# A graph kernel whose degrees are counted with ScalarE's one-hots, and whose first norms and messages are spread out

## The chip, the cores and the metric

The kernel runs on one core of one Trainium2 chip. The metric is the time of one launch on the device in microseconds (us). The core has five engines that run side by side and wait for each other by semaphores: TensorE (PE; its weight loads are shown apart as PEld), VectorE (DVE), ScalarE (ACT), GpSimd (POOL) and SyncE (SP). Each runs its instructions in the order in which they stand in its queue.

## The reference: what is computed

There are 6250 nodes with 128 features and 100000 edges, sorted by their destination. Each edge has a source, a destination and one of 8 types. First comes a relational graph network of three layers. In a layer, each edge fetches the row of its source under its type, weighs it by one over the number of edges that share its destination and type, and adds it to its destination:

```
h = einsum('ni,rio->nro', x, weight)        # one row per node and type
msg = h[src, etype]
norm = 1.0 / max(count of edges with the same (dst, etype), 1)
agg = segment_sum(msg * norm, dst)
x = agg + x @ root + bias                   # then batch norm and relu, but for the last layer
```

Between the two networks, and behind the second, a sum with the input is normalized by rows. The second network has no types and works with the degrees of the sources:

```
deg = segment_sum(1, src)
w = rsqrt(deg[src]) * rsqrt(deg[dst])
repeat 3 times: cur = segment_sum(cur[dst] * w, src); acc += cur
out = (acc / 4) @ W_out + b_out
```

## The kernel before

**The tiles.** The edges stand in 782 tiles of 128 (NTS). The first 192 (HT) belong to the first destinations, where many edges meet. Of these, tiles 0 to 91 (T1) are not gathered: dense_sums() (L1325) works them off as a multiplication with a table of counts. Tiles 92 to 191 are summed by first_sums() (L1087), and tiles 192 to 781 by window_sums() (L1644).

**A pass.** Each of the three layers is one pass. Its first part is first_sums(): for each of 100 tiles, GpSimd starts an indirect DMA (L1064) that fetches 128 rows of x into one of 27 buffers named gt, PE multiplies them with weighted one-hots o (L1067), which DVE makes for eight tiles at a time (one_hots(), L1052), and DVE adds the product to z (joined(), L1095). Beside it run the messages (messages(), L968): for each of 49 blocks of nodes two multiplications of 512 columns (L972), each copied by ScalarE (L973), and a store of 512 KB on SP's queue (L974) into the table h_d in DRAM; behind them 13 multiplications with root (L985). `nodes` is this generator, stepped in proportion to the tiles done: all 62 steps over the first `HN` = 66 tiles. The second part is window_sums(): 590 tiles, gathered from h_d, so it needs all the stores. Its products are added to agg (L1655). Between the passes stands a batch norm (L1697 to L1719).

**The norms.** The weight of each edge needs counts along rows of sorted edges. shares() (L814) is a chain of some 70 DVE operations with comparisons, scans in both directions and a few transposes by PE. It runs twice: for the edges of the first 208 tiles ("x", on rows of 256, L938), and for all the edges (on rows of 1024) within others() (L1031), a generator of 33 steps that also makes the gather indices gidx and the local columns lo. In layer 0 others() is stepped once per tile of first_sums(), from the fifth tile on (beside_layer_0, L1118). weights() (L674) makes the weight of a layer out of four bases, in 32 DVE operations of 128 columns.

**Work for later, beside the gathers.** The tables that dense_sums() and the last part need are built meanwhile by side_work() (L1613), a generator that window_sums() steps by take_turns() (L1640) in proportion to the tiles, over all three passes. It has three parts:

- hot_counts() (L1156): 62 steps for the table c1_d of the first destinations. dense_sums() needs it, which begins after 400 tiles of a pass's second part (DENSE_FROM).
- degrees() (L1404): how many edges each source has. For each of 196 groups of four tiles (TS), DVE compares 128 columns (lo_hot, L1419) and 49 columns (blk_hot, L1422) with the two parts of the source's number, both as one-hots of bf16, and PE multiplies the one with the other (L1431), adding up all 782 tiles in one PSUM tile pd. dis, the inverse root, is made of it.
- counts() (L1443): 12 steps of setting up with long DVE operations and PE multiplications in fp32 (L1507, L1529), then 1232 steps, one for each tile of a reordered list: a row (L1587), one-hots dst_hot for four tiles (L1583), two PE multiplications (L1601), an addition (L1560), and a store to a_d.

Before, one step of hot_counts() is followed by three of degrees(); then come the rest of degrees() and counts(). pd is also the sixth accumulator of dense_sums(), so degrees() must have ended before the first dense_sums() (L1674).

**The last part** (from L1736) multiplies with the table a_d, three times, and normalizes.

**What sets the order.** The program is written as generators, but a scheduler of the framework lays out each engine's queue: an instruction goes ahead as soon as its operands are expected. pin() (L749) ties an instruction to the pinned one before it on the same engine, so that pinned instructions keep the order of the text. Before, the one-hots, the gather multiplications, the joined additions and the steps of the side work are pinned; shares(), others(), checks() and weights() are not. GpSimd's queue holds almost nothing but gathers, in the order of the tiles.

Of the kernel before, what the change touches and what calls it, by code (L numbers as in the profile page):

```python
# [17 lines left out]
P = 128  # L18
# [501 lines left out]
def sorted_path(  # L520
# [60 lines left out]
    HW = 7  # L581
# [10 lines left out]
    DENSE_FROM = 400  # L592

# [163 lines left out]

    def rsqrt(pool, o, v, shape, name):
# [55 lines left out]
    def shares(x_, q, w, dst_x_, typ, to, j, meanwhile):  # L814
# [6 lines left out]
        nc.vector.tensor_tensor(same, dst_x_[:, : w + 1], dst_x_[:, 1:], op=OP.is_equal)  # L821
        nc.vector.tensor_scalar(at_first, at, at[:, 0:1], None, op0=OP.is_equal)
        yield
        nc.vector.tensor_scalar(at_last, at, at[:, w - 1 : w], None, op0=OP.is_equal)
        nc.vector.tensor_scalar(pair, typ, 2.0, None, op0=OP.is_ge)
        yield
        for k in range(2, KP):
            nc.vector.scalar_tensor_tensor(pair, typ, 2.0 * k, pair, op0=OP.is_ge, op1=OP.add)
        yield
        nc.vector.scalar_tensor_tensor(odd, pair, -2.0, typ, op0=OP.mult, op1=OP.add)  # L830
        nc.vector.tensor_scalar(unit, odd, 4095.0, 1.0, op0=OP.mult, op1=OP.add)
        yield
        ms = [m0, m1, m2, m3]
        for k, m in enumerate(ms):
            nc.vector.memset(m[:, w:], 0.0)
            nc.vector.scalar_tensor_tensor(m[:, :w], pair, float(k), unit, op0=OP.is_equal, op1=OP.mult)
            if k % 2:
                yield
        edge_cnt = [sp.tile([q, KP], F32, name=f"edge_cnt{x_}{k}") for k in range(2)]
        through = [sp.tile([q, KP], F32, name=f"through{x_}{k}") for k in range(2)]  # L840
        for i, mask in ((0, at_last), (1, at_first)):
            for k in range(KP):
                u = sp2.tile([P, W], F32, name="u")[:q, :w]
                nc.vector.scalar_tensor_tensor(u, ms[k][:, :w], 1.0, mask, op0=OP.mult, op1=OP.mult,
                                               accum_out=edge_cnt[i][:, k : k + 1])
                if k % 2:
                    yield
            nc.vector.tensor_tensor(through[i], at_last[:, 0:1].to_broadcast([q, KP]),
# [9 lines left out]
        for k in range(2):  # L858
            pq = pqs[k]
            flow = sp.tile([KP, 2 * P], F32, name=f"flow{x_}{k}")  # L860
            nc.vector.tensor_copy(flow.rearrange("p (k q) -> p k q", k=2)[:, :, :q],
                                  pq.rearrange("p (k q) -> p k q", k=2)[:, :, :q])
            run = sp.tile([KP, q + 2], F32, name=f"run{x_}{k}")
            nc.vector.memset(run, 0.0)
# [3 lines left out]
            nc.vector.tensor_tensor_scan(to_, keep, add, 0.0, op0=OP.mult, op1=OP.add)  # L868
            if k == 0 and w == W:

                full = sp.tile([KP, q], F32, name="full")
                nc.vector.scalar_tensor_tensor(full[:, : q - 1], keep[:, : q - 1], 1.0, keep[:, 1:],
# [8 lines left out]
        for k in range(2):  # L881
            b = sp.tile([q, KP], F32, name=f"before_row{x_}{k}")
            nc.vector.tensor_copy(b, pbs[k])
            before_row.append(b)
        meanwhile(2)
        for k in range(KP):
            f = sp2.tile([P, W], F32, name="u")[:q, :w]
            b = sp2.tile([P, W], F32, name="u")[:q, :w]
            nc.vector.tensor_tensor_scan(f, same[:, :w], ms[k][:, :w], before_row[0][:, k : k + 1], op0=OP.mult,
                                         op1=OP.add)  # L890
            yield
            nc.vector.tensor_tensor_scan(b[:, ::-1], ms[k][:, w:0:-1], same[:, w:0:-1],
                                         before_row[1][:, k : k + 1], op0=OP.add, op1=OP.mult)
            yield
            nc.vector.tensor_tensor(f, f, b, op=OP.add)
            if k == 0:
                nc.vector.scalar_tensor_tensor(total, pair, float(k), f, op0=OP.is_equal, op1=OP.mult)
            else:
                nc.vector.scalar_tensor_tensor(f, pair, float(k), f, op0=OP.is_equal, op1=OP.mult)
                nc.vector.tensor_tensor(total, total, f, op=OP.add)  # L900
# [3 lines left out]
        nc.vector.tensor_copy(hi_i, total)  # L904
        nc.vector.tensor_scalar(hi_i, hi_i, 12, None, op0=OP.logical_shift_right)
        nc.vector.tensor_copy(hi, hi_i)
        yield
        nc.vector.scalar_tensor_tensor(low, hi, -4096.0, total, op0=OP.mult, op1=OP.add)
        nc.vector.tensor_sub(hi, hi, low)
        yield  # L910
        nc.vector.tensor_mul(hi, hi, odd)
        nc.vector.tensor_add(total, low, hi)
        nc.vector.tensor_scalar_max(total, total, 1.0)
# [4 lines left out]
        nc.vector.reciprocal(to, to)  # L918
# [76 lines left out]
    def checks():  # L995

        skip = wide_tiles["at_last"][:Q, :W]
        nc.vector.scalar_tensor_tensor(skip, dst_f[:, :W], 0.0, dst_f[:, 1 : W + 1], op0=OP.add,
# [951 lines left out]
```

## Time and profile before

| what | us |
|---|---|
| median of 3 runs (3580.69 to 3591.91) | 3583.28 |
| the profiled execution | 3580.38 |
| its span | 3578.5 |
| first gather from h_d in layer 0, 1, 2, at | 199.66, 1184.71, 2119.13 |
| busy in the span: PE, DVE, ACT, POOL | 2714.5, 2272.8, 324.2, 2114.9 |
| last gather, at | 2879.17 |

A group of the profile is one line of the kernel on one engine: its operation, what it writes and reads, how often, its busy time and its mean in ns; behind the second bar the time for which the engine stood idle just before it, with what it waited for. A line of the timeline gives the start, the duration, engine, line and operation, and in brackets the idle time before it. A line of the windows gives busy time and number of instructions of each engine in one stretch, then the granted clock of PE as a share of full speed, the share of the DMA engines and GB/s. A line of the waits gives the sum, how many there were, and the longest.

### The profile page before, as it was taken

How to read it: one execution, taken by the hardware profiler on the slowest of the kernel's cores; microseconds unless marked ns; L12 is line 12 of the kernel's file. 1: busy time of each engine (PE TensorE's matmuls, PEld its weight loads, DVE VectorE, ACT ScalarE, POOL GpSimd, SP SyncE). 2: the span in 40 equal slices, each digit the busy share in tenths (PEclk: the TensorE clock that was granted, in tenths of full speed). 3: DMA queues.
4: the chain of work that ended last, by engine and by line, in shares of the span. 5: the costliest groups of instructions: out<-in, count | busy, mean ns of one | idle time of the engine just before them, and what ended most of it. 6: DMA issues, size and time to landing. Idle time of an engine off the chain costs nothing.

```text
span 3578.5 us, 53292 instructions
## 1 busy us (share of the span) xinstructions
PE 2714.5 (76%) x17110; PEld 2167.3 (61%) x17110; DVE 2272.8 (64%) x6623; ACT 324.2 (9%) x600; POOL 2114.9 (59%) x2083
## 2 busy tenths in 40 slices
PE   5976667677659766666765986666677679999998
PEld 3464455655545555555544565555555569999997
DVE  7678896953752766666456357666653566656566
ACT  3500000001025000000100520000001020000000
POOL 6577777677757777777776667777777710000000
PEclk9955556558569555555765985555567579999999
DMA  6611122123238222222322852222233234545442
GB/s 194 230 52 50 52 61 70 45 66 97 59 115 313 64 66 68 68 71 73 100 69 58 297 184 78 76 77 78 76 86 79 68 97 135 158 131 157 133 139 80
DMA packets 422807, 373.23 MB, mean 104 GB/s; under 512 B 89934, under 2 KB 370286, under 8 KB 422516
## 3 DMA queue, kind: packets, MB, share of 16 engines
q1 hardware_dynamic: 347832, 230.32, 21.0%
q0 software_dynamic: 66240, 135.79, 13.5%
q10 hardware_dynamic: 8444, 3.61, 0.4%
q8 instruction: 136, 2.23, 0.3%
q14 instruction: 155, 1.27, 0.1%
HBM read 250.74 MB, written 178.62 MB: 120 GB/s over the span
## 4 chain that ended last, share of the span: by engine, by line
PE 39%; DMA 37%; DVE 11%; issue 7%; POOL 5%; DVEq 0%; POOLq 0%; ACT 0%; ACTq 0%
DMA gt<-h_d,gidx 37%; PE pw L1865 15%; PE pw L972 7%; PE ps L1067 6%; POOL gt L1064 5%; PE pw L1368 3%; PE pw L1601 2%; DVE row L1587 2%; DVE had L1560 1%; PE pw L1395 1%; PE pw L985 1%; DVE dst_hot L1583 1%; DVE agg L1655 1%; PE ps L1823 1%; PE pd L1368 1%
## 5 line engine op out<-in xcount | busy, mean ns | idle before, releaser
L1064 POOL DMA_INDIRECT gt<-h_d,gidx x1770 | 1797.9, 1016 | 554.1 <-DMA gt<-h_d,gidx 221.8
L1067 PE MATMUL ps<-o,gt 128*128 128x48 f32 (+1 forms) x4140 | 1148.3, 391 | 666.8 <-DMA gt<-h_d,gidx 590.9
L1067 PEld LDWEIGHTS ps<-o,gt 128*128 128x128 f32 x4140 | 947.5, 290 | 954.2 <-DMA gt<-h_d,gidx 779.2
L1587 DVE TENSOR_SCALAR row<-iota_c,e_tab,e_tab 128x252 bf16<-128x252 int16 x1232 | 421.6, 350 | 326.2 <-PE pw L1601 324.3
L1865 PE MATMUL pw<-three,u 128*128 128x193 bf16 x7203 | 615.8, 248 | 14.2 <-issue 9.9
L1865 PEld LDWEIGHTS <-u 128*128 128x128 fp8e3 x7203 | 602.4, 98 | 21.8 <-issue 10.0
L1601 PE MATMUL pw<-dst_hot,row 128*126 128x128 bf16 x2464 | 411.9, 318 | 56.8 <-DVE row L1587 51.9
L1601 PEld LDWEIGHTS <-row 128*126 128x126 bf16 x2464 | 337.1, 225 | 74.3 <-DVE row L1587 64.1
L1560 DVE SCALAR_TENSOR_TENSOR had<-had,keep,pw 126x256 int32<-126x256 int32 x616 | 292.1, 474 | 1.9 <-PE pw L1601 1.8
L972 PE MATMUL pw<-w,xT 128*128 128x512 f32 x588 | 288.8, 622 | 0.0
L1064 POOL DMA_INDIRECT gt<-x_d,xidx x200 | 195.0, 975 | 133.7 <-DMA xc<-in_x_dram 31.9
L1655 DVE TENSOR_TENSOR agg<-agg,ps 128x48 f32 x885 | 178.6, 202 | 141.6 <-PE ps L1067 107.3
L1859 DVE TENSOR_SCALAR u<-packed 128x640 int32<-128x640 int32 (+1 forms) x243 | 127.0, 522 | 201.9 <-PE pw L1865 200.1
L1583 DVE TENSOR_TENSOR dst_hot<-iota_f,e_tab 128x512 bf16<-128x512 f32 x308 | 211.5, 687 | 0.0
L1095 DVE TENSOR_TENSOR z<-z,ps 128x56 f32 x300 | 63.0, 210 | 194.2 <-PE ps L1067 182.3
L973 ACT COPY hs<-pw 128x512 f32<-128x512 f32 x294 | 171.7, 585 | 141.3 <-PE pw L972 134.4
L1368 PE MATMUL pw<-x,u 128*128 128x385 bf16 x735 | 178.3, 385 | 6.6 <-DVE had L1560 3.3
L1064 POOL DMA_INDIRECT gt<-in_x_dram,xidx x100 | 119.3, 1193 | 77.3 <-PE ps L1067 46.3
L972 PEld LDWEIGHTS pw<-w,xT 128*128 128x128 f32 x588 | 106.1, 197 | 86.9 <-issue 80.7
L1419 DVE TENSOR_TENSOR lo_hot<-iota_f,e_tab 128x512 bf16<-128x512 f32 x196 | 134.3, 685 | 32.4 <-PE pd L1431 31.3
L1368 PEld LDWEIGHTS <-u 128*128 128x128 fp8e3 x882 | 101.3, 119 | 79.7 <-issue 40.5
L1056 DVE TENSOR_TENSOR o<-iota_f,lo 128x384 f32<-128x384 f32 x222 | 122.7, 553 | 41.0 <-PE ps L1067 41.0
(396 smaller groups left out, 1890.8 us busy)
## 6 DMA issues: line engine op xcount, KB each, us to landing
a_d<-had SPq DMA_DIRECT2D x616, 126.0 KB
h_d<-hs SPq DMA_DIRECT2D x147, 512.0 KB
packed<-a_d SPq DMA_DIRECT2D x135, 320.0 KB
packed<-a_d SPq DMA_DIRECT2D x108, 384.0 KB
gt<-h_d,gidx POOLq DMA_INDIRECT x1770, 2.5
c_d<-had SPq DMA_DIRECT2D x62, 196.0 KB
packed<-c_d SPq DMA_DIRECT2D x21, 448.0 KB
x_d<-xc SPq DMA_DIRECT2D x24, 256.0 KB
```

The costliest lines, as they stand in the source:

```text
L972: nc.tensor.matmul(ph, xT[:, b * P : (b + 1) * P], w[:, c : c + 512], start=True, stop=True)
L973: nc.scalar.copy(hs[:, c : c + 512], ph)
L1064: nc.gpsimd.indirect_dma_start(out=gt, out_offset=None, in_=table[:, :], in_offset=bass.IndirectOffsetOnAxis(ap=at[:, t : t + 1], axis=0))
L1067: pin(nc.tensor.matmul(pa, gt, o, start=first_, stop=last))
L1368: nc.tensor.matmul(sums[d][:, :C3D], us[d % 2][:, i, :, d // 2], x3[:, i, :], start=(c == 0 and i == 0), stop=(c * CH + i == NBLK - 1))
L1419: pin(nc.vector.tensor_tensor(hot[:, :n, :], iota_f[:, None, :].to_broadcast([P, n, P]), src_lo[:, t0 : t0 + n, None].to_broadcast([P, n, P]),
L1560: pin(nc.vector.scalar_tensor_tensor(now[:HB, : 2 * P], had[:HB, : 2 * P], keep[:HB, s : s + 1], p[:HB, : 2 * P], op0=OP.mult, op1=OP.add))
L1583: pin(nc.vector.tensor_tensor(hots[i // TS], iota_f[:, None, :].to_broadcast([P, TS, P]), flat(e_lo)[:, i : i + TS, None].to_broadcast([P, ...
L1587: pin(nc.vector.tensor_scalar(rows[i][:, : 2 * HB], iota_c[:, : 2 * HB], e_col[:, s, j : j + 1], e_val[:, s, j : j + 1], op0=OP.is_equal, ...
L1601: pin(nc.tensor.matmul(sums[s][:HB, c * P : (c + 1) * P], row[:, c * HB : (c + 1) * HB], hots[u // TS][:, u % TS, :], start=(j == 0 and c ...
L1655: pin(nc.vector.tensor_add(to, to, pa))
L1865: nc.tensor.matmul(out_of(f), bytes_[f % 2][:, d, :, f // 2], cur[:, b, :], start=(b == 0 and f % 2 == 0), stop=(c0 == NSL - 1 and d == m ...
```

## The change

Four things are changed.

1. degrees() makes its one-hots on ScalarE: the absolute difference of a column number and the source's part, for 128 and for 49 columns of one tile (Abs), then one Relu of 1 minus that for four tiles. It sums DEG = 4 groups (16 tiles) in pd at a time and adds pd to deg on DVE. It works in two halves of the tiles, and uses the memory of e_src.
2. side_work() leaves hot_counts() at one step in four, with nothing in the other three, then starts counts(), and steps degrees() once per step of counts() from step 12 on. dense_sums() waits for an open group of degrees() only (close_degrees).
3. In layer 0 the messages and the root multiplications spread over HT - T1 - 8 = 92 tiles instead of 66, and others() is stepped in two of five tiles instead of in each.
4. All DVE operations of shares(), checks(), others() and of the first weights are pinned by `in_order`. The first weights are made by 7 operations of 1024 columns.

In the next layers the messages still take 66 tiles.

```diff
+    class Pinned:
+        def __getattr__(self, name):
+            return lambda *args, **kw: pin(getattr(nc.vector, name)(*args, **kw))
+
+    in_order = Pinned()
...
-        nc.vector.tensor_tensor(same, dst_x_[:, : w + 1], dst_x_[:, 1:], op=OP.is_equal)
+        in_order.tensor_tensor(same, dst_x_[:, : w + 1], dst_x_[:, 1:], op=OP.is_equal)
...
-    w0 = weights(0, bases_0)
+    w0 = wp.tile([P, R * D], F32, name="w")
+    w0_r = w0.rearrange("p (r d) -> p r d", r=R)
+    comp_0 = comp_b[:, : R * NB].rearrange("p (r b) -> p r b", b=NB)
+    for b in range(NB):
+        to = w0_r if b == 0 else sp2.tile([P, W], F32, name="u").rearrange("p (r d) -> p r d", r=R)
+        in_order.tensor_tensor(to, bases_0[:, b, None, :].to_broadcast([P, R, D]),
+                               comp_0[:, :, b, None].to_broadcast([P, R, D]), op=OP.mult)
+        if b:
+            in_order.tensor_tensor(w0_r, w0_r, to, op=OP.add)
...
     def beside_layer_0(k):
-        for _ in range(1 if k >= 4 else 0):
+        if k >= 4 and k % 5 in (0, 2):
             next(other_tiles, None)
 
-    first_sums(0, layer_0, NBLK + NC, HN, beside_layer_0)
+    first_sums(0, layer_0, NBLK + NC, HT - T1 - 8, beside_layer_0)
...
     def degrees():
...
+        HALF = -(-NTS // 2)
+        room = flat(e_src)
+        src_lo, src_blk = room[:, :HALF], room[:, HALF : 2 * HALF]
+        for h in range(2):
+            of = gidx[:, h * HALF : h * HALF + HALF]
...
+            for t0 in range(begin, end + TS, TS):
+                n = min(TS, end - t0)
+                if n > 0:
+                    near = cp.tile([P, TS, P + NBLK], BF16, name="near")
+                    for j in range(n):
+                        k = t0 - begin + j
+                        nc.scalar.activation(near[:, j, :P], iota_b, AF.Abs, bias=src_lo[:, k : k + 1], scale=-1.0)
+                        nc.scalar.activation(near[:, j, P:], iota_b[:, :NBLK], AF.Abs,
+                                             bias=src_blk[:, k : k + 1], scale=-1.0)
+                        yield
+                    nc.scalar.activation(near[:, :n, :], near[:, :n, :], AF.Relu, bias=ones[:, :1], scale=-1.0)
+                    made[t0] = near, n
+                if t0 > begin:
+                    near, n = made.pop(t0 - TS)
+                    step = (t0 - TS - begin) // TS
+                    first_, last = step % DEG == 0, step % DEG == DEG - 1 or t0 >= end
+                    if first_:
+                        pd = ps_d.tile([P, 512], F32, name="pd")
+                    for j in range(n):
+                        pin(nc.tensor.matmul(pd[:, :NBLK], near[:, j, :P], near[:, j, P:],
+                                             start=first_ and j == 0, stop=last and j == n - 1))
+                    if last:
+                        if h == 0 and step < DEG:
+                            pin(nc.vector.tensor_copy(deg, pd[:, :NBLK]))
+                        else:
+                            pin(nc.vector.tensor_add(deg, deg, pd[:, :NBLK]))
+                    open_degrees[0] = not last
...
     def side_work():
-        others = degrees()
         for _ in hot_counts():
+            for _ in range(3):
+                yield
+        counted[0] = True
+        others = beside[0] = degrees()
+        for k, _ in enumerate(counts()):
+            if k >= 8 + 2 * TU:
+                next(others, None)
             yield
-            for _ in range(3):
-                if next(others, "end") != "end":
-                    yield
-        counted[0] = True
         for _ in others:
             yield
-        degrees_known[0] = True
-        for _ in counts():
-            yield
-    N_SIDE = 6 + NS1 + 2 + 2 + -(-NTS // TS) + 1 + 5 + 2 * TU + 3 + NST * TU + LEAD
+
+    def close_degrees():
+        while open_degrees[0]:
+            next(beside[0])
+
+    N_SIDE = 3 * (6 + NS1 + 2) + 5 + 2 * TU + 3 + NST * TU + LEAD
...
                 finish_sums[0]()
-                assert counted[0] and degrees_known[0]
+                close_degrees()
+                assert counted[0]
                 dense = dense_sums(l, w)
```

## The prediction, made before the changed kernel was run

> **What bounds the kernel now.** The page first: GpSimd (POOL) is busy only 59% of the span, but those 2115 us lie ahead of about 2880 us, where the multiplications of the last part (L1865) begin.
>
> ```profile
> span 3578.5 us, 53292 instructions
> ...
> PE 2714.5 (76%) x17110; PEld 2167.3 (61%) x17110; DVE 2272.8 (64%) x6623; ACT 324.2 (9%) x600; POOL 2114.9 (59%) x2083
> ...
> L1064 POOL DMA_INDIRECT gt<-h_d,gidx x1770 | 1797.9, 1016 | 554.1 <-DMA gt<-h_d,gidx 221.8
> ```
>
> All but a few of POOL's waits in front of a gather are 0.3 us long (221.8 us are 728 waits, the longest 0.3), which is what one gather needs before the next: POOL was not held up, it is the bound. In the timeline of POOL the 590 gathers from h_d take 823 us in layer 0 (199.66 to 1023), 767 in layer 1 (1184.71 to 1951) and 761 in layer 2 (2119 to 2880). The same work is 57 us dearer in layer 0, and the windows show where:
>
> ```profile
> core 0: us, PE busy (x) PEld busy (x) DVE busy (x) ACT busy (x) POOL busy (x), PEclk, DMA share, GB/s
> 57.00:168.00 111.00, 102.26 (x300) 51.28 (x301) 80.72 (x159) 58.06 (x100) 57.47 (x52) 0.92 0.70 259
> 215.00:585.00 370.00, 238.48 (x1440) 182.43 (x1440) 325.18 (x869) 2.67 (x4) 291.99 (x256) 0.50 0.20 57
> 1185.00:1690.00 505.00, 339.33 (x1594) 279.97 (x1594) 346.77 (x1018) 0.00 (x0) 386.77 (x389) 0.50 0.25 69
> ```
>
> From 215 to 585 us, while degrees() runs, a gather comes every 370/256 = 1.445 us; in layer 1, beside counts(), every 505/389 = 1.298 us. VectorE (DVE) is 88% and 69% busy there, ScalarE (ACT) nearly idle. The groups of POOL in these two windows give the gather itself:
>
> ```profile
> L1064 POOL DMA_INDIRECT gt<-h_d,gidx x256 | 292.1, 1141 | 78.0 <-DMA gt<-h_d,gidx 39.3 <-issue 25.6 <-PE ps L1067 6.7
> L1064 POOL DMA_INDIRECT gt<-h_d,gidx x389 | 387.2, 995 | 118.5 <-DMA gt<-h_d,gidx 44.8 <-issue 34.4 <-PE pw L1601 31.7
> ```
>
> An undisturbed gather takes 0.94 us. The timeline shows what stretches one: this one began at 551.16, and DVE ran one comparison with two inputs in SBUF after the other, without a pause:
>
> ```profile
> 551.03 0.68 DVE L1419 TENSOR_TENSOR lo_hot<-iota_f,e_tab 128x512 bf16<-128x512 f32 x1
> 551.64 0.35 DVE L1422 TENSOR_TENSOR blk_hot<-iota_f,e_tab 128x196 bf16<-128x196 f32 x1
> 551.91 0.68 DVE L1419 TENSOR_TENSOR lo_hot<-iota_f,e_tab 128x512 bf16<-128x512 f32 x1
> ...
> 551.16 3.73 POOL L1064 DMA_INDIRECT gt<-h_d,gidx  x1 [0.30 <-DMA gt<-h_d,gidx]
> ```
>
> It ended only after 554.57, when DVE came to an operation that reads PSUM (L1312).
>
> **A rule weighed against this.** The Trainium skill, "SBUF — State Buffer", section "Who interferes with whom", has VectorE and GpSimd share one pair of ports, locked by either for a whole instruction; it names tensor_tensor with both inputs in SBUF. Taken by the letter, the lock is free again after every instruction, so a gather could lose at most one comparison, 0.69 us: with 382 of them over 256 gathers and half an operation (0.26 us) lost each time at 55% of DVE's time, some 0.14 us per gather, or 37 us. The row shows 2.79 us lost at once under a closed run of them, so loss goes by runs, not by instructions. Both leave the excess at 256 x (1.445 - 1.298) = 38 us; they differ on what is left when DVE stays nearly as busy with other work, and there layer 1's 1.298 is measured, so I use that.
>
> **The change, part by part.**
>
> *Degrees' comparisons leave DVE.* 196 x (0.687 + 0.355) = 204 us of DVE work go, nearly all between 211 and 573 us. hot_counts() keeps its one step in four turns, now with nothing in the other three, and counts() starts some 215 tiles into the pass instead of some 270; after that a turn holds one step of counts(), 1457/1460 = 1.00 against 1516/1460 = 1.04 before, so layer 0 gets the DVE mix that layer 1 has. 590 x 1.300 = 767 us. On top comes what layer 1 doesn't have, the setting up of counts(): PE runs 92 fp32 multiplications in a row (592 to 645 us) and POOL waited 15.0 us for a buffer. The planned order of the changed kernel has that run unbroken as well, with four short operations of degrees() more in DVE's queue (about 2 us): 17 us. Slow first tiles beside the set-up of hot_counts(), +5; then hot_counts() alone, 210 tiles at an estimated 0.02 us less than beside counts() (DVE some 2.7 us in 5.2 instead of 69%), -4. So 785 instead of 823: **38 us gained** (30 to 50).
>
> *ScalarE takes them.* 782 tiles, each an Abs of 128 and one of 49 columns, and a Relu of 708 for four tiles. The nearest rows have a bias per partition too:
>
> ```profile
> L991 ACT ACTIVATE agg<-pw,bias_c 128x512 f32<-128x512 f32 x12 | 8.2, 687 | 4.8 <-PE pw L985 4.8
> ...
> L991 ACT ACTIVATE agg<-pw,bias_c 128x128 f32<-128x128 f32 x1 | 0.4, 359 | 0.0
> ```
>
> That is 0.25 us and 0.85 ns per column: 0.36 + 0.29 + 0.86/4 = 0.86 us per tile, 676 us in all, against a tile's 1.30 us. ScalarE has no other work inside a pass (0.00 in the window of layer 1), so all of it is hidden; POOL, PE and DVE do not wait as long as it stays under 1.30. Lower bound, 0.20 us for an Abs (bn_a, one column, L762): 0.6 us per tile; upper bound, 0.687 for an Abs: 1.6, which would be 784 x 0.3 = 235 us lost. The 128-column row is the very width, so I take 0.86. The page "ScalarE: Activation LUTs", section "Rules for kernel authors", speaks against the change: relu and the like belong on VectorE, up to three times faster per element. Here it is 0.26 us on DVE against 0.86 on ACT, so by the rule the change loses 782 x 0.6 = 470 us of engine time. It is no loss of span: DVE's 0.26 stretches the bound engine, ACT's 0.86 touches nothing.
>
> *PE's part* stays 782 multiplications at about 0.07 us pitch (four in 0.37 to 0.53 us), now one tile in each turn: PE goes from 67% to some 73% in these stretches. PE's order is fixed, so it would stand at a near tile that is late; the Relu is placed a group of four (5.2 us) ahead of its multiplications and ScalarE needs 3.5 us for a group: cost 0, covered by 27 buffers, 35 us of gathers.
>
> *49 additions of PSUM into deg* on DVE, 0.2 us each (agg, L1655), 10 us in all. Each waits for the PE's newest multiplication; behind it on DVE stand the next row (L1587) and the had addition. DVE has 0.4 us of slack per turn, 6 us per 16 tiles; a wait of 1 to 3 us fits: 0. On SP the 62 stores of c1_d and the 616 of a_d keep their order; the last of c1_d leaves near 465 us, and dense_sums() reads it after 400 tiles, near 700 us: 0. The finishing of an open group ahead of dense_sums() is at most 16 tiles of ScalarE, 14 us, twice: under the 35 us. At the end of layers 0 and 1 up to 16 tiles of ScalarE stand ahead of the first hs copies, and the load of the square root's table comes in layer 0's normalization: 0 to 2 us each, 2 in all.
>
> *First pass of layer 0.* Its 100 gathers end at 199.66, though 100 x 1.29 would be 129 us. POOL's waits there:
>
> ```profile
> POOL gt L1064 <- PE ps L1067: 47.2, 28, 13.1
> ```
>
> PE frees the buffers late, because it makes the messages (busy 102 of the 111 us of the first window above): the last of 196 halves ended at 168.0, and POOL, at gather 76 then, needed 25 more. PE's sum from the start of messages (57.5) is 98 x 0.857 + 37 tiles x 0.33 + transposes 2 = 98 us; 12 more are waits. In the changed order all 49 transposes of x come before anything else, the chain for the first norms is 5 us shorter (18 foreign operations leave it, 6 us, and pinning costs 1), w is 7 x 1.2 us instead of 32 short operations (10 us), but DVE stands some 8 us at the zeroing of the last x buffer. Messages start near 49.5; the 16 tiles that PE did before them (7.4 us) come later. Last message: 49.5 + 84 + 56 x 0.33 + 2 = 154, with 0 to 13 us of waits, taken as 5: 159. By then 56 tiles are freed instead of 52, POOL is at gather 83, and 17 x 1.45 later (DVE's chain of 76 us now lies beside the last gathers) the first gather from h_d goes out at 184 to 187. SP's stores of h_d end 20 us earlier than that and are no bound. The norms are ready near 184: their readers are PE's window tiles, with 27 gathers of cover. **13 us gained** (-5 to 20).
>
> Sum against the profiled execution (3580.4 us; 3578.5 of span and 1.9 around it): -38 - 13 + 2 - 2 (layers 1 and 2 with 4% fewer DVE steps, 58 us of excess over 0.94) = -51. The median shown is 2.9 us above that execution, so 3583.3 - 51 = **3532**.
>
> **Rivals.**
> 1. *The pins bite.* With one fixed order on DVE and on PE, each waits for the other in the first 200 us: tiles 72 to 99 stand behind the norm chain, whose scans are 2.4 us each. The 13 us are lost or turn to -9: 3545 to 3563, about 3554. For it: PE already waits 16.1 us for a norm (L913) at the start. Against: only 17 gathers lie behind it. Chance 0.16.
> 2. *The change does not lighten the gathers*: counts() in the first pass locks as much as degrees() did, pitch near 1.42. Then 13 us remain: 3570. Against it stand 390 gathers of layer 1. Chance 0.07.
> 3. *Slower: ScalarE becomes the pace.* If one tile costs it x > 1.30 us, PE stands at each group (queued behind it: the gather multiplications, and for their buffers POOL), 784 x (x - 1.30) us. From x = 1.365 it eats the 51 us. With the fixed part of an activation doubled to 0.5 us, x is 1.43 and the time 3583 + 102 - 51 = 3634. Against: 0.86 from the rows. Chance 0.09.
>
> **How the numbers follow.** Likeliest 0.68, own range 3515 to 3548 (gathers 30 to 50, first pass 5 to 20). The range goes up to rival 1's end and a part of rival 2 and down to both gains at their best, 3510 to 3568. A difference within 0.3% (11 us) is about what a measurement of this kernel can't tell from no change. Faster: likeliest, rival 1 and half of rival 2, 0.87; within: 0.05; slower: 0.08.
>
> **What would show it.** Right: 590 gathers from h_d of layer 0 in 775 to 795 us, with a mean near 1.0 us and no gather over 2.5 us between 220 and 560; the first one near 185; ACT busy near 1000 us, each tile about 0.8 us; layers 1 and 2 unchanged within 5 us; the last part from L1865 on as long as before. Wrong: PE waiting for ACT at the degrees' multiplications in total over 50 us, a pitch over 1.36 in layer 0, or a first gather from h_d after 200 us.

## The result and the profile after

The changed kernel takes 3529.2 us (median, 3523.1 to 3530.6), the kernel before 3585.8 us beside it: a ratio of 0.9837, 95% interval 0.9825 to 0.985. The forecast was 3532. All ratios below are to the kernel before, run beside the kernel in question on the same chip; but for one chip its median was 3585.6 to 3586.5 us. The profiled execution has a span of 3528.1 us against 3578.5. First the page of the changed kernel, its span, busy times and the row of the gathers (busy and mean ns, then the idle time before them):

```profile
span 3528.1 us, 54660 instructions
...
PE 2695.5 (76%) x17110; PEld 2161.4 (61%) x17110; DVE 2125.9 (60%) x6259; ACT 916.4 (26%) x2360; POOL 2083.9 (59%) x2083
...
L1080 POOL DMA_INDIRECT gt<-h_d,gidx x1770 | 1768.9, 999 | 546.8 <-DMA gt<-h_d,gidx 235.6
```

DVE lost 147 us of work, ACT took on 592 (916.4 - 324.2), and a gather became 17 ns shorter on average. GpSimd (POOL) still sets the pace: most of its waits in front of a gather are again 0.3 us (us in total, times, longest):

```profile
POOL gt L1080 <- DMA gt<-h_d,gidx: 235.6, 773, 0.3
```

Its timeline, cut at the first and last gather of each pass, shows where 50 us went:

| stretch on POOL, us | before | forecast | after |
|---|---|---|---|
| start to first gather from h_d | 199.7 | 184 to 187 | 182.7 |
| 590 gathers from h_d, layer 0 | 823.4 | 785 | 783.1 |
| boundary to layer 1 | 31.6 | up to +2 | 32.6 |
| x gathers, layer 1 | 130.1 | same | 127.9 |
| 590 gathers from h_d, layer 1 | 766.7 | about -1 | 775.0 |
| boundary to layer 2 | 31.9 | up to +2 | 32.0 |
| x gathers, layer 2 | 135.8 | same | 136.0 |
| 590 gathers from h_d, layer 2 | 761.0 | about -1 | 757.7 |
| rest | 698.4 | same | 701.0 |

Layer 1 is the one row that went the other way. The windows of the changed kernel: the first two as in the prediction, the last one the stretch of layer 1 in which degrees() now runs beside counts():

```profile
core 0: us, PE busy (x) PEld busy (x) DVE busy (x) ACT busy (x) POOL busy (x), PEclk, DMA share, GB/s
57.00:168.00 111.00, 106.42 (x376) 58.31 (x374) 82.92 (x153) 58.58 (x100) 78.00 (x63) 0.97 0.71 264
215.00:585.00 370.00, 261.36 (x1081) 195.45 (x1079) 246.06 (x708) 54.78 (x164) 278.67 (x275) 0.54 0.22 62
...
1140.00:1655.00 515.00, 358.65 (x1984) 303.62 (x1984) 343.99 (x1015) 303.29 (x895) 395.81 (x392) 0.50 0.24 68
```

In the first window POOL makes 63 gathers where it made 52. In the second DVE is busy 67% instead of 88%, and a gather comes every 370/275 = 1.345 us instead of 1.445; the window holds the setting up of counts(), so it is not the steady pace, which is 320/246 = 1.30 from 640 to 960 us. In layer 1 it comes every 515/392 = 1.314, against 1.298 before, although DVE is less busy (66.8% against 68.7%).

### The profile page after: what moved, and what is told of

It is laid out like the page before. It is cut to its first block, busy times and chain, and to the rows that moved or that the text cites. A ratio compares the mean times of both kernels' runs of the same rounds, so it can differ in the third digit from the quotient of the medians.

```text
span 3528.1 us, 54660 instructions
## 1 busy us (share of the span) xinstructions
PE 2695.5 (76%) x17110; PEld 2161.4 (61%) x17110; DVE 2125.9 (60%) x6259; ACT 916.4 (26%) x2360; POOL 2083.9 (59%) x2083
## 4 chain that ended last, share of the span: by engine, by line
PE 41%; DMA 37%; DVE 10%; issue 6%; POOL 5%; ACT 0%; DVEq 0%; POOLq 0%; ACTq 0%
DMA gt<-h_d,gidx 36%; PE pw L1899 16%; PE pw L979 7%; PE ps L1083 7%; POOL gt L1080 5%; PE pw L1384 2%; PE pw L1630 2%; DVE row L1616 1%; PE pw L1411 1%; PE pw L992 1%; DVE had L1589 1%; DVE agg L1688 1%; PE ps L1857 1%; PE pw L1558 0%; DVE dst_hot L1612 0%
## 5 line engine op out<-in xcount | busy, mean ns | idle before, releaser
L1080 POOL DMA_INDIRECT gt<-h_d,gidx x1770 | 1768.9, 999 | 546.8 <-DMA gt<-h_d,gidx 235.6
L1083 PE MATMUL ps<-o,gt 128*128 128x48 f32 (+1 forms) x4140 | 1136.3, 389 | 638.1 <-DMA gt<-h_d,gidx 562.1
L1083 PEld LDWEIGHTS ps<-o,gt 128*128 128x128 f32 x4140 | 936.5, 289 | 928.8 <-DMA gt<-h_d,gidx 752.3
L1899 PEld LDWEIGHTS <-u 128*128 128x128 fp8e3 x7203 | 602.9, 98 | 22.6 <-issue 10.0
L1442 ACT ACTIVATE near<-iota_b,e_tab 128x128 bf16<-128x128 bf16 x782 | 304.7, 391 | 747.7 <-PE pd L1455 443.6
L1630 PE MATMUL pw<-dst_hot,row 128*126 128x128 bf16 x2464 | 447.5, 320 | 54.1 <-DVE row L1616 49.5
L1630 PEld LDWEIGHTS <-row 128*126 128x126 bf16 x2464 | 353.9, 224 | 66.8 <-DVE row L1616 57.2
L1443 ACT ACTIVATE near<-iota_b,e_tab 128x49 bf16<-128x49 bf16 x782 | 250.5, 321 | 0.0
L1358 ACT CAST x<-xc 128x512 bf16<-128x512 f32 x21 | 13.0, 621 | 673.5 <-PE pw L1384 541.5
L1446 ACT ACTIVATE near<-near,ones 128x708 bf16<-128x708 bf16 x196 | 172.9, 882 | 5.7
```

What stands on the lines that cost most here:

```text
L1080: nc.gpsimd.indirect_dma_start(out=gt, out_offset=None, in_=table[:, :], in_offset=bass.IndirectOffsetOnAxis(ap=at[:, t : t + 1], axis=0))
L1083: pin(nc.tensor.matmul(pa, gt, o, start=first_, stop=last))
L1442: nc.scalar.activation(near[:, j, :P], iota_b, AF.Abs, bias=src_lo[:, k : k + 1], scale=-1.0)
L1443: nc.scalar.activation(near[:, j, P:], iota_b[:, :NBLK], AF.Abs, bias=src_blk[:, k : k + 1], scale=-1.0)
L1630: pin(nc.tensor.matmul(sums[s][:HB, c * P : (c + 1) * P], row[:, c * HB : (c + 1) * HB], hots[u // TS][:, u % TS, :], start=(j == 0 and c ...
L1899: nc.tensor.matmul(out_of(f), bytes_[f % 2][:, d, :, f // 2], cur[:, b, :], start=(b == 0 and f % 2 == 0), stop=(c0 == NSL - 1 and d == m ...
```

## The experiments

### The two halves apart: the first pass alone, degrees() alone

```diff
 e1: the kernel before, plus
+    in_order = Pinned()
+        if k >= 4 and k % 5 in (0, 2):
+    first_sums(0, layer_0, NBLK + NC, HT - T1 - 8, beside_layer_0)
 e2: the kernel before, plus
+                        nc.scalar.activation(near[:, j, :P], iota_b, AF.Abs, bias=src_lo[:, k : k + 1], scale=-1.0)
+            if k >= 8 + 2 * TU:
+                next(others, None)
```

> The kernel before, with only the first pass of layer 0 changed (norm chain and first weights pinned in order, spread over its tiles); degrees' comparisons stay on VectorE in layer 0. Theory (two independent gains): first gather from h_d near 183 us, then 590 gathers in about 823 us as before; 17 us gained, about 3567 us. Rival (the first pass gains only because the side work behind it changed too): first gather near 199 us, about 3584 us.

> The kernel before, with only degrees() changed: ScalarE makes the comparisons over all passes, the first pass as before. Theory: first gather from h_d at 199.7 us as before, layer 0's 590 gathers in 783 to 787 us, layer 1's some 8 us longer than before; 3584 - 40 + 8 = about 3550 us. Rival (the gathers of layer 0 gained because the first pass leaves another state behind): layer 0 near 823 us, about 3580 us.

Measured: the first pass alone 3573.0 us, ratio 0.9965 (0.9951 to 0.9979); degrees() alone 3545.6, ratio 0.9884 (0.9869 to 0.9899). The first gather from h_d goes out at 183.0 us with the first pass changed, and at 204.4 with only degrees() changed. Layer 0's 590 gathers take 827.4 and 781.4 us. By the ratios the gains are 12.6 and 41.6 us and add up to 54; together they gave 58, within the intervals. So there are two independent gains, as the first theory said. Layer 1 is again longer (776.7) where degrees() is changed, not where the first pass is (766.6).

### Inside the first pass: pins or spread

```diff
 e6: the changed kernel, minus the pins
-    in_order = Pinned()
+    in_order = nc.vector
 e7: the changed kernel, minus the spread
-        if k >= 4 and k % 5 in (0, 2):
-            next(other_tiles, None)
+        for _ in range(1 if k >= 4 else 0):
+            next(other_tiles, None)
-    first_sums(0, layer_0, NBLK + NC, HT - T1 - 8, beside_layer_0)
+    first_sums(0, layer_0, NBLK + NC, HN, beside_layer_0)
```

> The changed kernel with the norm chain, checks and first weights unpinned (the planner may place them), still spread over the first pass. In PE's order the last message is then after 72 tiles instead of 56 and all transposes of x are no longer first. Theory (the pins with the transposes first give most of the first pass's gain): messages end near 165 us, first gather from h_d at 192 to 200 us, 10 to 17 us slower than the changed kernel: 3539 to 3546 us. Rival (the spread alone gives it): first gather near 184 us, 3530 us.

> The changed kernel with the pins kept, but the messages again on the first 66 tiles and one step of the norm chain in every tile. Theory (pins and transposes first give most; the spread takes the norm chain's waits off PE): last message after 48 tiles but PE waits for the chain's VectorE work again; messages end near 155 us, first gather from h_d near 187 us, some 4 us slower than the changed kernel: 3533 us. Rival (the spread is the gain): near 199 us, 3545 us.

Measured: without pins 3526.3 us, ratio 0.9835 (0.9822 to 0.9848), first gather from h_d at 182.1. Without the spread 3556.9 us, ratio 0.992 (0.9906 to 0.9933), first gather at 215.8, which is 16 us later than in the kernel before. The theory fell both times. The pins, the transposes ahead of everything and an early start of the messages are worth nothing measurable: without pins the messages begin at 66.6 us and end at 172.8, later than before (168.1), and POOL still arrives at 182. The spread is what the gain needs, and pins without it cost time. Two things were not taken apart. Both kernels keep the first weights in 7 operations, so what those are worth is not known; and the spread is two edits, the messages over 92 tiles and others() in two of five, which were only tried together.

The waits of POOL in the first pass show why; us in total, times, longest. The changed kernel:

```profile
POOL gt L1080 <- PE ps L1083: 26.3, 19, 9.4
```

The kernel without the spread:

```profile
POOL gt L1080 <- PE ps L1083: 57.6, 22, 20.3
```

The kernel with the spread but without pins:

```profile
POOL gt L1076 <- PE ps L1079: 29.9, 32, 15.8
```

Before it was 47.2. Messages and gather multiplications share PE in one fixed order. Spread over 66 tiles, about one step of the messages and the root stands behind each tile; over 92, two behind three tiles. So more tiles stand ahead of the last message: 56 in the changed kernel and 72 without pins, against 52 before and 48 without the spread. POOL, which its 27 buffers let run ahead of PE, was at gather 79, 95, 77 and 70 when the last message ended, and each gather that was left then took 1.3 to 1.9 us. An even mix is not what makes it: with pins PE has up to 54 multiplications of messages in a row (60 without the spread), without them mostly 4 between two or four of gathers, before as well.

### Is it ScalarE, or the place and the pace?

```diff
 e10: the changed kernel, degrees' comparisons back on VectorE
-                        nc.scalar.activation(near[:, j, :P], iota_b, AF.Abs, bias=src_lo[:, k : k + 1], scale=-1.0)
...
-                    nc.scalar.activation(near[:, :n, :], near[:, :n, :], AF.Relu, bias=ones[:, :1], scale=-1.0)
+                    pin(nc.vector.tensor_tensor(near[:, :n, :P], iota_f[:, None, :].to_broadcast([P, n, P]),
+                                                src_lo[:, k : k + n, None].to_broadcast([P, n, P]), op=OP.is_equal))
...
```

> The changed kernel with degrees' two comparisons per four tiles back on VectorE (two inputs in SBUF), at the changed kernel's places and pace: one group per four turns, over all passes; everything else as changed. Theory (runs of VectorE's two-input SBUF operations hold the gathers): the gathers beside degrees() lengthen; the same edit, on a chip where GpSimd did not set the pace, raised the excess of all 1770 gathers over 0.94 us from 78 to 113 us, so at least 35 us are lost where GpSimd does: 3560 to 3600 us. Rival (the gain came from degrees' new place and pace, not from the engine): 3529 us, layer 0's 590 gathers still in 783 us.

Measured: 3547.4 us, ratio 0.9898 (0.9883 to 0.9913). So the change of engine is worth 0.6%, 18 to 22 us. The remaining 37 to 39 us stay when the comparisons are made by VectorE: 13 to 17 of them are the first pass, 20 to 26 the new place and pace. Neither theory was right. Layer 0 takes 794.1 us, so 29 of its 40 us come without ScalarE; but most of the comparisons have left that layer: 128 of the 392 are made beside its gathers, where before all of them were, and 250 beside those of layer 1, which take 776.5 us, 1.5 more than in the changed kernel. The window of layer 1 shows how little they cost there:

```profile
core 0: us, PE busy (x) PEld busy (x) DVE busy (x) ACT busy (x) POOL busy (x), PEclk, DMA share, GB/s
...
1160.00:1650.00 490.00, 338.95 (x1867) 286.10 (x1866) 401.98 (x1148) 0.00 (x0) 377.54 (x370) 0.50 0.24 67
```

DVE is 82% busy, and a gather still comes every 490/370 = 1.324 us. In the kernel before, DVE at 88% gave 1.445. What differs can be read gather by gather from the timelines, by what DVE is doing when a gather begins. A gather that begins while DVE is idle, or runs an operation that reads one tensor in SBUF at most, takes 0.95 us on average. One that begins while DVE runs an operation with two tensors in SBUF ends, as a rule, 0.82 us after that operation does (0.818 on average, with a standard deviation of 0.003), or is not stretched where less than 0.12 us of it is left. "Held longer" counts those that ended more than 0.05 us later than that; 4 to 12 in each window ended earlier. The excess is over 0.943 us, in us for all these gathers together:

| window | gathers | begun in a two-input operation | of these held longer | excess up to the end of that operation | excess beyond it |
|---|---|---|---|---|---|
| before, 215 to 585 | 256 | 164 | 30 | 28.4 | 22.1 |
| degrees back on DVE, 1160 to 1650 | 369 | 173 | 10 | 25.2 | 2.5 |
| changed, 1140 to 1630 | 372 | 96 | 0 | 24.1 | 0 |
| before, 1200 to 1690 | 377 | 101 | 0 | 18.7 | 0 |

In the first row a gather pays in two ways. More than half of the excess is the rest of the one operation that was running; 22 us are waits over several. There degrees() put three groups of comparisons on four tiles, which made closed runs; with one group in four tiles and other operations between, such waits are nearly gone. Why 30 gathers waited over several operations and 130 did not is open. Rows 3 and 4 have no such wait, so layer 1's 8 us are not a matter of runs: as many gathers begin in a two-input operation, but with more of it still to come (0.43 us on average, against 0.34). Why they begin earlier in it is open too.

### The operand's place

```diff
 e11: the changed kernel
+    pd_all = ps_d.tile([P, 512], F32, name="pd")
+    iota_ps = pd_all[:, 448:].bitcast(BF16)
+    nc.vector.tensor_scalar(pd_all[:, 448:].bitcast(I32), iota_b.bitcast(I32), 0, None, op0=OP.bitwise_or)
...
-        pin(nc.vector.tensor_tensor(o[:, :n, :width], iota_f[:, None, :width].to_broadcast([P, n, width]),
+        pin(nc.vector.tensor_tensor(o[:, :n, :width], iota_ps[:, None, :width].to_broadcast([P, n, width]),
...
-                    pin(nc.vector.tensor_tensor(hots[i // TS], iota_f[:, None, :].to_broadcast([P, TS, P]),
+                    pin(nc.vector.tensor_tensor(hots[i // TS], iota_ps[:, None, :].to_broadcast([P, TS, P]),
```

> The changed kernel with a bf16 copy of the numbers 0 to 127 kept in PSUM, and the comparisons of dst_hot in counts() and of the gathers' one-hots o reading it instead of the SBUF copy. Theory: VectorE's operations then have one input in SBUF only and leave the gathers alone; the excess of 1770 gathers, 102 us in the changed kernel, falls by half, 40 to 60 us gained: 3470 to 3490 us. Rival (the operand's place doesn't matter, VectorE's time does): within 5 us of 3529 us.

Measured: 3468.7 us, ratio 0.9676 (0.9663 to 0.969). It beats both kernels, by about 117 us and 60. Layers 0, 1 and 2 take 767.1, 742.8 and 747.0 us. The group of the gathers in the changed kernel, 1140 to 1630 us:

```profile
L1080 POOL DMA_INDIRECT gt<-h_d,gidx x373 | 377.5, 1012 | 113.7 <-DMA gt<-h_d,gidx 42.7 <-issue 33.5 <-PE pw L1630 27.4
```

The groups of VectorE and POOL in this one, 1130 to 1600 us:

```profile
L1615 DVE TENSOR_TENSOR dst_hot<-pd,e_tab 128x512 bf16<-128x512 bf16 x95 | 64.9, 683 | 0.1
...
L1075 DVE TENSOR_TENSOR o<-pd,lo 128x384 f32<-128x384 bf16 x48 | 26.4, 550 | 0.0
...
L1083 POOL DMA_INDIRECT gt<-h_d,gidx x376 | 356.5, 948 | 114.6 <-DMA gt<-h_d,gidx 43.3 <-issue 28.6 <-PE pw L1633 20.7
```

The same comparisons take the same time (683 ns against 687), in the same order, and the gather is back at 0.948 us. So it is not VectorE's time that stretches a gather. The 80 gathers that begin during dst_hot or o take 0.95 us at most here, where in the changed kernel those that begin during dst_hot take 1.25 on average; and 8 that begin during o times norm, which still reads two tensors in SBUF, take 1.08. All this speaks for the second operand read from SBUF. One rival was not tried: the copy in PSUM is also bf16, the one in SBUF fp32, and no run read a bf16 copy from SBUF. The Trainium skill, "SBUF — State Buffer", section "Who interferes with whom", says that a VectorE instruction with at most one SBUF input outside its two-port modes leaves GpSimd alone; these rows agree. One caution on this kernel: the copy lies in the bank that degrees' multiplications write, and in its timeline a multiplication into it waits for the comparison. "PSUM — Partial Sum Buffer", section "Summary: rules for kernel authors", asks for a different bank where PSUM is read while a matmul runs; no run here tried without that wait, and a kernel to keep should give the copy its own bank.

### The same question on a chip where GpSimd is not the bound

Four kernels ran on another chip, on which the kernel before took 4054.4 us. Its numbers are compared with nothing else.

```diff
 c4: the changed kernel, with pd_all and iota_ps as above, read by nothing
 e3: c4, with degrees' comparisons on VectorE
+                    pin(nc.vector.tensor_tensor(near[:, :n, :P], iota_f[:, None, :].to_broadcast([P, n, P]),
...
 e8: e3, with
-                    pin(nc.vector.tensor_tensor(near[:, :n, :P], iota_f[:, None, :].to_broadcast([P, n, P]),
+                    pin(nc.vector.tensor_tensor(near[:, :n, :P], iota_ps[:, None, :].to_broadcast([P, n, P]),
...
 e9: c4, with
-                    pin(nc.vector.tensor_tensor(hots[i // TS], iota_f[:, None, :].to_broadcast([P, TS, P]),
+                    pin(nc.vector.tensor_tensor(hots[i // TS], iota_ps[:, None, :].to_broadcast([P, TS, P]),
```

> The changed kernel, with the one PSUM bank of degrees() held as one tile for the whole program and a bf16 copy of the numbers 0 to 127 in its last quarter, which nothing reads here. It is the base for the next three. Expected by all: 3529 us as the changed kernel, within 5 us.

> As the base, but degrees' two comparisons per four tiles go back to VectorE (two inputs in SBUF), in the changed kernel's places, one group per four turns over all passes. Theory (a gather is held by runs of VectorE's two-input SBUF operations): 782 tiles times 0.26 us more VectorE work beside counts(); by before's first window (88% busy, +0.147 us per gather against 69%) the some 780 gathers beside them lose up to 0.14 us each; 40 to 110 us lost, 3570 to 3640 us. Rival (the gain comes from degrees' new place and pace, not from the engine): 3529 us.

> As the kernel with degrees' comparisons on VectorE, but the numbers 0 to 127 that they compare with are read from PSUM. VectorE does the same operations for about the same time. Theory (what stretches a gather is the shared SBUF port while VectorE reads two SBUF inputs): most of the loss against the base is gone, gathers' mean back to about 1.01 us, 3530 to 3550 us. Rival (VectorE's busy time itself delays PE and with it the buffers): no better than with SBUF inputs.

> As the base, with ScalarE doing degrees' comparisons, and the 308 comparisons of dst_hot in counts() reading the numbers 0 to 127 from PSUM instead of SBUF. Theory: excess of the gathers over 0.94 us, 40 us in layer 0, 40 in layer 1, 23 in layer 2, falls by the share of dst_hot among the operations with two SBUF inputs (67 of about 122 us per 500), 30 to 50 us gained in all: 3480 to 3500 us. Rival (row and had hold the gathers as much): less than 10 us gained.

Measured: 4039.5, 4031.9, 4060.9 and 4043.5 us, ratios 0.9967 (0.9948 to 0.9986), 0.9951 (0.9927 to 0.9976), 1.0012 (0.9985 to 1.0038) and 0.9962 (0.9938 to 0.9985). The times expected were for a chip on which GpSimd sets the pace, and none of the theories' times was met. The timeline of POOL in the first of them tells why (idle before a gather in brackets):

```profile
1608.37 0.94 POOL L1083 DMA_INDIRECT gt<-h_d,gidx  x1 [0.52 <-issue]
1609.61 0.94 POOL L1083 DMA_INDIRECT gt<-h_d,gidx  x1 [0.30 <-issue]
1612.01 0.94 POOL L1083 DMA_INDIRECT gt<-h_d,gidx  x1 [1.45 <-remote]
```

Every 9 to 15 us POOL stands still for 1.2 to 2.2 us, and partly the other engines with it (of 200 us from 1600 on, 18 have no engine busy, against 1 of 200 in the changed kernel from 1400 on); 590 gathers take 872 to 957 us. In the four rows below, the busy time of the gathers and the idle time before them add up to 2700 to 2733 us: a shorter gather was followed by a longer wait. What pauses that chip stays open: the trace names no releaser inside the core ("remote", "issue"). But the gathers' own lengths can be read (row of the page: busy and mean ns, idle before). The base c4:

```profile
L1083 POOL DMA_INDIRECT gt<-h_d,gidx x1770 | 1745.0, 986 | 970.9 <-issue 361.7
```

With degrees' comparisons on VectorE, both inputs in SBUF (e3):

```profile
L1083 POOL DMA_INDIRECT gt<-h_d,gidx x1770 | 1775.4, 1003 | 924.9 <-issue 355.8
```

The same with the numbers in PSUM (e8):

```profile
L1083 POOL DMA_INDIRECT gt<-h_d,gidx x1770 | 1744.0, 985 | 988.7 <-issue 378.1
```

The base with dst_hot's numbers in PSUM (e9):

```profile
L1083 POOL DMA_INDIRECT gt<-h_d,gidx x1770 | 1716.8, 970 | 1003.8 <-issue 381.5
```

Degrees' comparisons on VectorE add 30 us to the gathers (the expectation for e10 above counts 35), with the numbers read from PSUM none, and dst_hot from PSUM takes 28 off.

### What ScalarE's work costs

```diff
 e4: the changed kernel
-                        nc.scalar.activation(near[:, j, :P], iota_b, AF.Abs, bias=src_lo[:, k : k + 1], scale=-1.0)
...
-                        pin(nc.tensor.matmul(pd[:, :NBLK], near[:, j, :P], near[:, j, P:],
+                        pin(nc.tensor.matmul(pd[:, :NBLK], iota_b, iota_b[:, :NBLK],
 e5: the changed kernel, both Abs lines twice
+                        nc.scalar.activation(near[:, j, :P], iota_b, AF.Abs, bias=src_lo[:, k : k + 1], scale=-1.0)
+                        nc.scalar.activation(near[:, j, P:], iota_b[:, :NBLK], AF.Abs,
+                                             bias=src_blk[:, k : k + 1], scale=-1.0)
```

> The changed kernel without ScalarE's comparisons for degrees(): the same 782 multiplications and 49 additions are made, but from constant tiles, so the degrees and what follows from them are left wrong. It shows what ScalarE's 730 us cost beside the gathers. Theory as predicted (they touch nothing): 3529 us, layers 0 and 1 in 783 and 775 us. Rival (ScalarE's work beside the gathers is what made layer 1 longer by 8 us than before): layer 1 back to about 766 us, layer 0 near 775 us, 3512 us.

> The changed kernel with every Abs of degrees() made twice: ScalarE needs 2 x (0.391 + 0.321) + 0.883 / 4 = 1.645 us per tile instead of 0.932. Theory (nothing is lost below the gathers' pitch, and 782 x the excess above it): 782 x (1.645 - 1.31) = 262 us lost, about 3790 us, with PE waiting for near at L1455. Rival (ScalarE's work is cushioned over the passes and stays hidden): 3530 to 3560 us.

Without ScalarE's part the whole took 13574.6 us: after the fast part the program computed everything again by its general path (its gathers from h_d at L387 are not in the fast part), so this time says nothing on the question. The fast part still ran first, and its rows can be read. Its 1770 gathers:

```profile
L1080 POOL DMA_INDIRECT gt<-h_d,gidx x1770 | 1767.8, 999 | 546.8 <-DMA gt<-h_d,gidx 224.3
```

That is the changed kernel's 1768.9 and 999; layers 0 and 1 take 783.2 and 773.1 us. ScalarE's work costs the gathers 2 us at most, and it is not what made layer 1 longer.

With the Abs made twice the kernel takes 3551.7 us, ratio 0.9901 (0.9887 to 0.9916): 22 us lost, not 262. The term that failed is the cost of a tile, 1.645 us, a sum of durations. The timeline of ScalarE in the changed kernel:

```profile
1300.14 0.32 ACT L1443 ACTIVATE near<-iota_b,e_tab 128x49 bf16<-128x49 bf16 x1
1300.37 0.39 ACT L1442 ACTIVATE near<-iota_b,e_tab 128x128 bf16<-128x128 bf16 x1
1300.66 0.32 ACT L1443 ACTIVATE near<-iota_b,e_tab 128x49 bf16<-128x49 bf16 x1
1300.88 0.39 ACT L1442 ACTIVATE near<-iota_b,e_tab 128x128 bf16<-128x128 bf16 x1
```

An Abs begins while the one before is still ending: 0.29 and 0.22 us from start to start, where the durations say 0.39 and 0.32. A tile occupies ScalarE for 592/782 = 0.76 us, and with doubled Abs for 0.76 + 0.51 = 1.27, still under the gathers' 1.31. In that kernel ScalarE is busy 250.5 of 260 us (1400 to 1660), and PE does stand at degrees' multiplications:

```profile
PE pd L1458 <- ACT near L1449: 167.4, 86, 4.6
```

Yet layers 0 and 1 take 782.7 and 772.1 us, no more than in the changed kernel: these 167 us of PE were not on the path, with no wait over 4.6 us and 27 buffers ahead. The 22 us lie in the x gathers of layer 1, 148.7 us instead of 127.9. There the planned order has more of degrees' operations ahead of the first copies of hs, which begin at 1010.3 instead of 1004.0, and PE makes gather multiplications alone until 1030.

## Why the prediction was right, and where it was not

*The sum.* -38 in layer 0's gathers was -40.3, -13 in the first pass was -17, +2 at the boundaries was +1.1. Layers 1 and 2, put at -2, gave +8.3 and -3.3. The total of -51 was -50.4, with +0.7 from the x gathers of layers 1 and 2 and the last part, put at nothing. The sum of the parts was sound, but that it met the time within 3 us is luck: layers 1 and 2 came out 7 us worse than forecast, layer 0, the first pass and the boundaries together 7 us better. Three of the reasons did not hold.

*"Degrees' comparisons leave DVE": size right, cause half right.* For most of the gain the comparisons had to leave layer 0's gathers, not VectorE: with two thirds of them moved to later layers but still on DVE, 29 of the 40 us come anyway (e10), and over the whole kernel place and pace are worth about as much as the engine. "Loss goes by runs, not by instructions" was read from one gather. The rule weighed there, one operation at most, accounts for 28.4 us of the excess between 215 and 585 us (the prediction's sum for it was 37), and waits over several for 22.1. Nor need that gather have waited for the operation that reads PSUM: it ended 0.83 us after the last comparison did, at 554.06, which is the step of the others. The longest gather between 220 and 560 us is now 2.0 us, as foretold (under 2.5). The set-up of counts() cost POOL 7.8 us in place of 15.0; its 17 were too much.

*"Layers 1 and 2 with 4% fewer DVE steps": wrong sign in layer 1.* It counted DVE's operations. Layer 1 has fewer of them, but the gathers' excess over 0.94 us rose from 32.7 to 41.0 us. ScalarE is ruled out (e4), and with the comparisons' operand in PSUM the same work leaves 8.7 us (e11). By the table the gathers begin earlier within the operations that hold them; no kernel changed that alone.

*"ScalarE takes them", 0.86 us per tile: hidden as said, but mis-sized.* It occupies 0.76 us, since the price was a sum of durations that overlap. PE waited for ScalarE at degrees' multiplications for 1.6 us in all, against the 50 named as a sign of being wrong; that sign was itself unsound, since 167 us of such waits cost the gathers from h_d nothing (e5). So rival 3's point of decision, 1.365 us, has to be taken from start to start; at 1.27 us the passes showed no loss (e5), and what lies above was not tried. The rule of "ScalarE: Activation LUTs", section "Rules for kernel authors", stays beside the point here: the engine time lost was not on the path.

*"First pass of layer 0": time right, mechanism wrong.* Messages began at 49.8 us (49.5 foretold) and ended at 151.1 (159), and the first gather from h_d came at 182.7 (184 to 187). But the step built this on the messages' early end, by the transposes going first, the shorter chain and the cheaper w. Without the pins the messages end at 172.8, and nothing is lost (e6); w stayed cheap there, and was not tried apart. What the step booked as a side effect, 56 tiles freed by the last message instead of 52, is the part that the runs bear out: with 72 POOL arrives as early, with 48 it comes 16 us later than before (e6, e7).

*Rivals.* The pins did bite, as rival 1 had it, but only without the spread: 215.8 us (e7). Rival 2 fell with layer 0's pitch of 783.1/590 = 1.33 (it named 1.42), rival 3 with the 0.76 us per tile.

## What to carry to other kernels

When VectorE stretches GpSimd's gathers, look at how often a gather begins during an operation with two SBUF inputs, and at closed runs of these, not at how busy VectorE is. Moving and spreading such operations was worth here about as much as giving them to another engine, and reading one operand of the others from PSUM took off another 60 us. Where two kinds of work share one in-order engine that frees another engine's buffers, look at how much of the second kind is done when the first ends, not at how early it ends. For an engine's limit use the time from start to start, since the durations in a profile may overlap.

## What the runs showed of the hardware

- *What holds a gather.* In the four windows of the table, gathers that began outside VectorE's operations with two tensors in SBUF took 0.945 to 0.954 us on average, those that began inside 1.10 to 1.25. With dst_hot's and o's numbers in PSUM (bf16), 10 of 375 began inside one, and the mean was 0.948.
- *For how long.* Mostly until the operation that was running ends, and 0.82 us more. One gather below begins during o, which ends at 1408.34, and ends at 1409.16, though o times norm has begun at 1408.37; the one before begins outside such operations, the one behind it with 0.07 us of dst_hot left. POOL's timeline in the changed kernel:

```profile
1406.57 0.94 POOL L1080 DMA_INDIRECT gt<-h_d,gidx  x1 [0.30 <-DMA gt<-h_d,gidx]
1407.82 1.34 POOL L1080 DMA_INDIRECT gt<-h_d,gidx  x1 [0.30 <-DMA gt<-h_d,gidx]
1409.46 0.94 POOL L1080 DMA_INDIRECT gt<-h_d,gidx  x1 [0.30 <-issue]
```

VectorE's, in the same time:

```profile
1407.79 0.55 DVE L1072 TENSOR_TENSOR o<-iota_f,lo 128x384 f32<-128x384 f32 x1
1408.37 0.56 DVE L1074 TENSOR_TENSOR o<-o,norm 128x384 f32<-128x384 f32 x1
1408.85 0.68 DVE L1612 TENSOR_TENSOR dst_hot<-iota_f,e_tab 128x512 bf16<-128x512 f32 x1
1409.45 0.34 DVE L1616 TENSOR_SCALAR row<-iota_c,e_tab,e_tab 128x252 bf16<-128x252 int16 x1
```

- *Sometimes over a run, and not for one that comes first.* In the kernel before, the gather of 3.73 us that began at 551.16, inside a closed run, ended 0.83 us after the run's last comparison, the second line below. One that began 0.01 us ahead of a comparison took 0.95, though two more comparisons followed without a pause:

```profile
548.67 0.72 DVE L1419 TENSOR_TENSOR lo_hot<-iota_f,e_tab 128x512 bf16<-128x512 f32 x1
553.65 0.41 DVE L1293 TENSOR_TENSOR dst_hot<-iota_f,e_tab 128x256 bf16<-128x256 f32 x1
...
548.66 0.95 POOL L1064 DMA_INDIRECT gt<-h_d,gidx  x1 [0.30 <-DMA gt<-h_d,gidx]
```

- *One chip of those used ran the kernel before in 4054 us*, and there the change (with an idle tile more, c4) was worth 0.3% instead of 1.6%, while GpSimd no longer set the pace. The last part took the same 698 us there as here. Why the passes pause is open.
